# Longer transfers in a one-core graph-attention kernel: x by eight blocks, results by four, the last block of adj in halves

## The chip, the cores and the metric

The kernel runs on one core of one Trainium2 chip. The metric is the device time of one execution in microseconds; lower is better. A core has five engines that are named here as the profile names them: PE (TensorE, with its weight loads as PEld), DVE (VectorE), ACT (ScalarE), POOL (GpSimd) and SP (SyncE, which here only issues transfers). Sixteen DMA engines move data between HBM and the core's memory.

## The reference

`x` is 4096 x 512, `adj` 4096 x 4096, `W` 512 x 2048 (four heads of 512 columns) and `a` holds two vectors of 512 for each head; all are float32.

```python
def _L0_gnn_ref(h, adj_mat, W, a):
    N = h.shape[0]
    ht = (h @ W).reshape(N, N_HEADS, N_HIDDEN).transpose(1, 0, 2)
    a_src = a[:, :N_HIDDEN, 0]
    a_dst = a[:, N_HIDDEN:, 0]
    src = jnp.einsum('hnd,hd->hn', ht, a_src)
    dst = jnp.einsum('hnd,hd->hn', ht, a_dst)
    e = jax.nn.leaky_relu(src[:, :, None] + dst[:, None, :], SLOPE) + adj_mat[None]
    att = jax.nn.softmax(e, axis=-1)
    h_prime = jnp.einsum('hij,hjd->hid', att, ht)
    return h_prime.mean(axis=0)

x = _layernorm(x + _L0_gnn_ref(x, adj, L0_gnn_W, L0_gnn_a), axis=-1)
```

The entries of adj are zero or between 0.05 and 1e9, and they are added to the scores. Where the largest entry of a row stands far above all others, the softmax puts its whole weight on that one column, whatever the heads say. The row's result is then the layer norm of `x[i] + x[j] @ mean_of_heads(W)`, with j the column of the row's largest entry.

## The kernel before

`leading_rows` computes all rows in this short way and tests on the way whether it holds for each row. `general` computes blocks of rows in full, and is entered only where the test finds a row for which the short way doesn't hold. The order of the instructions is written by hand: each engine works off its own list in the order in which the code records it.

The rows are cut into 32 blocks (`NB`) of 128; block `ib` takes row `p * 32 + ib` on partition `p`, so that consecutive blocks of x or of the output are contiguous for each partition: one block of x or of the output is 2 KB per partition, four are 8 KB and eight are 16 KB. A block of adj is 2 MB, 16 KB per partition.

The loop over `t` (L423) starts one block at each turn and carries earlier ones further:

- `load_adj(t + 5)` (L117) issues the block of adj that comes five turns later, into a pool of six buffers. Blocks 28 to 30 come in two pieces and block 31 in four (`pieces`, L114). `load_x` (L124) issues several blocks of x at once into `hold`, which holds all of x and later the results. All these, and the stores, are issued by SP in one queue, in the order of the code.
- `segment_maxima(t, ...)` (L162) has DVE reduce the block to one maximum for each segment of 16 or 32 columns. A block up to 30 is reduced in two instructions, block 31 in four, one for each piece. Between the first and the rest stands `find_column(t - 2)` (L210) of the block two turns earlier. At the last turn `middle` (L431) is 1, so one quarter of block 31 stands ahead of `find_column(29)` and three behind it.
- `find_segment(t)` (L174) has DVE find the largest segment. POOL then fetches that segment of each row ("lead", L191) by an indirect DMA. `find_column` two turns later has DVE find the place inside it, POOL computes the column (L216), and POOL fetches that row of x ("y", L202) by another indirect DMA. For block 31 the column is searched in the whole row instead (`find_column_in_row`, L219).
- `turn(t - 3)` (L225) transposes y on PE and copies it by ACT; `products` (L239) multiplies it by the mean of the heads of W and `residual` (L233) adds x. ACT computes the statistics (L263), POOL the factor (L270), and ACT writes the result to `hold` (L275).

Blocks 24 to 27 (`BEHIND` = 24, `LATE` = 28) are handled apart: their products are put by (L253), their x is loaded last, and x is added behind the loop, for 24 to 26 by POOL (`add_x(nc.gpsimd, ...)`, L261). The place of these adds in POOL's list matters for what follows. It is, after the gather of y for block 29: the add of block 24; column and y of block 30; row and lead of block 31; the add of block 25; y of block 31; the add of block 26 (L486 to L491).

Where x is loaded: blocks 0 to 3 ahead of the loop, behind the issue of adj 4 (L136), 4 to 11 at turn 3, 12 to 15 at turn 11, 16 to 23 at turn 15 (L418), 28 to 31 ahead of adj 31, and 24 to 27 at turn 31, in two pieces of two blocks (L440). Stores (L328) all stand behind the loop: 0 to 7 by four blocks, 8 to 23 by two (L482 to L485), and, when the rest of the code has been recorded, 28 and 29 one by one, 24 and 25 together, 26 and 27 together, 30, and 31 (L540 to L542).

A DMA of SP's queue takes one of eight semaphores in turn, and its issue waits until an earlier DMA on that semaphore has landed.

Of the kernel before, what the change touches and what calls it, by code (L numbers as in the profile page):

```python
# [13 lines left out]
OP = mybir.AluOpType  # L14
AX = mybir.AxisListType
# [53 lines left out]
def leading_rows(ctx, tc, x, adj, W, a, out, ident, v, n_bad, any_bad):  # L69
# [8 lines left out]
    nc = tc.nc  # L78
    N, D = x.shape
    H = a.shape[0]  # L80
    KB, NB, S = D // P, N // P, N // E
    S_EARLY = N // E_EARLY
    AHEAD = 5
    Q = 4
    PIECES = 4
    LATE = NB - Q
    BEHIND = LATE - Q

# [23 lines left out]
    adj_t = {}  # L112

    def pieces(ib):  # L114
        return PIECES if ib == NB - 1 else 2 if ib >= LATE else 1

    def load_adj(ib):  # L117
        if 0 <= ib < NB:
            t = adj_t[ib] = adj_pool.tile([P, N], F32, name="adj_t")
            n = pieces(ib)  # L120
            for k in range(n):
                nc.sync.dma_start(t[:, ts(k, N // n)], adj_rows[ib][:, ts(k, N // n)])

    def load_x(lo, n):  # L124
        nc.sync.dma_start(hold[:, ds(lo, n), :], x_rows[:, ds(lo, n), :])

    def load_w(kb):
        nc.sync.dma_start(hold[:, ds(w_at + kb * H, H), :], w_blocks[:, kb])
# [3 lines left out]
        nc.scalar.dma_start(a_rows[ts(s, H), :], a[:, ts(s, D), :].rearrange("h d o -> h (d o)"))  # L132
    for kb in range(KB):
        load_w(kb)
        load_adj(kb + 1)
    load_x(0, Q)  # L136
    for ib in range(KB + 1, AHEAD):
        load_adj(ib)

# [20 lines left out]
    seg_of, at_of, lead_of, y_t, yt_of, o_ps = {}, {}, {}, {}, {}, {}  # L160

    def segment_maxima(ib, lo, hi):  # L162

        e = E_EARLY if ib < EARLY else E
        if lo == 0:
            seg_of[ib] = small.tile([P, N // e], F32, name=f"seg{e}", bufs=2)
        n = max(pieces(ib), 2)
        for k in range(lo * n // PIECES, hi * n // PIECES):
            nc.vector.tensor_reduce(  # L169
                seg_of[ib][:, ts(k, N // e // n)],  # L170
                adj_t[ib][:, ts(k, N // n)].rearrange("p (s e) -> p s e", e=e), axis=AX.X, op=OP.max,
            )

    def find_segment(ib):  # L174
        seg = seg_of.pop(ib)
        nc.vector.max(out=top[:, ib, :], in_=seg)
        at = at_of[ib] = small.tile([P, 8], U32, name="at")
        nc.vector.max_index(at, top[:, ib, :], seg)  # L178
        if ib < NB - 1:
            fetch_segment(ib)  # L180
# [29 lines left out]
    def find_column(ib):  # L210
        if ib < BEHIND:
            find_inner(ib)
        within = small.tile([P, 8], U32, name="within")
        nc.vector.max_index(within, top[:, ib, :], lead_of[ib])  # L214
        col = small.tile([P, 1], U32, name="col")
        nc.gpsimd.tensor_tensor(col, at_of.pop(ib), within[:, 0:1], op=OP.add)  # L216
        gather_rows(ib, col)
# [7 lines left out]
    def turn(ib):  # L225
        y = y_t.pop(ib)
        tp = psum.tile([P, KB, P], F32, name="tp", bufs=2)
        for kb in range(KB):
            nc.tensor.transpose(tp[:, kb, :], y[:, ts(kb, P)], ident)  # L229
        yt = yt_of[ib] = rows.tile([P, KB, P], F32, name="yt")  # L230
        nc.scalar.copy(yt, tp)  # L231

    def residual(ib):  # L233
        start = ib not in o_ps
        if start:
            o_ps[ib] = psum.tile([P, D], F32, name="o")
        nc.tensor.matmul(o_ps[ib], ident, hold[:, ib, :], start=start, stop=False)  # L237
# [11 lines left out]
    def row_norm(ib):  # L249
        sq = rows.tile([P, D], F32, name="sq")  # L250
        nc.scalar.activation(sq, hold[:, ib, :], AF.Square, accum_out=xx[:, ib : ib + 1])  # L251
# [18 lines left out]
    def rstd(i):  # L270
        nc.gpsimd.tensor_scalar(sd[:, i], sd[:, i], 1.0 / D, EPS, op0=OP.mult, op1=OP.add)
        nc.gpsimd.tensor_tensor(sd[:, i], sd[:, i], power[:, : i.stop - i.start], op=OP.pow)  # L272
        nc.gpsimd.tensor_mul(nm[:, i], nm[:, i], sd[:, i])
# [54 lines left out]
    def store(queue, lo, n):  # L328
        queue.dma_start(out_rows[:, ds(lo, n), :], hold[:, ds(lo, n), :])

    def mean_of_heads(kb):
        o = psum.tile([P, D], F32, name="o")
        for h in range(H):
            nc.tensor.matmul(o, ident, hold[:, w_at + kb * H + h, :], start=(h == 0), stop=(h == H - 1))  # L334
        nc.scalar.activation(w_sum[:, kb, :], o, AF.Copy, scale=1.0 / H)  # L335
# [5 lines left out]
    def turn_a():  # L341
        tp = psum.tile([P, KB, P], F32, name="tp", bufs=2)
        for k in range(KB):
            nc.tensor.transpose(tp[:, k, : 2 * H], a_rows[:, ts(k, P)], ident[: 2 * H, : 2 * H])
        nc.scalar.copy(at_d, tp[:, :, : 2 * H])

    def turn_w(kb, h):
        tp = psum.tile([P, KB, P], F32, name="tp", bufs=2)
        for k in range(KB):
            nc.tensor.transpose(tp[:, k, :], hold[:, w_at + kb * H + h, ts(k, P)], ident)  # L350
        wt = rows.tile([P, KB, P], F32, name="wt")
        nc.scalar.copy(wt, tp)  # L352
        return wt

    def head_vector(kb, h, wt):

        for k in range(KB):
            nc.tensor.matmul(  # L358
                pv[:, kb, h : 2 * H : H], wt[:, k, :], at_d[:, k, h : 2 * H : H],
                start=(k == 0), stop=(k == KB - 1),  # L360
            )

    def head_norms():
        nc.vector.tensor_copy(v, pv)
        vv = once.tile([P, KB, 2 * H], F32, name="vv")
        nc.vector.tensor_mul(vv, v, v)
        pn = psum.tile([P, KB, 2 * H], F32, name="px", bufs=1)
        nc.tensor.matmul(pn, ones, vv, start=True, stop=True)
        n2 = once.tile([P, 2 * H], F32, name="n2")
        nc.vector.tensor_reduce(n2, pn.rearrange("p k c -> p c k"), axis=AX.X, op=OP.add)  # L370
        nc.scalar.activation(n2, n2, AF.Sqrt)
        both = once.tile([P, H], F32, name="both")
        nc.vector.tensor_add(both, n2[:, :H], n2[:, H:])
        nc.vector.tensor_reduce(vn, both, axis=AX.X, op=OP.max)
# [40 lines left out]
        nc.vector.tensor_reduce(total, pg, axis=AX.X, op=OP.add)  # L415
        nc.vector.tensor_scalar(any_bad, total, -1.0, float(N), op0=OP.mult, op1=OP.add)

    x_at = {Q - 1: (Q, 2 * Q), 3 * Q - 1: (3 * Q, Q), 4 * Q - 1: (4 * Q, 2 * Q)}  # L418
    vectors = [(kb, h) for kb in range(KB) for h in range(H)]
    vectors_at = {t: 2 if t < 3 else 1 for t in range(1, 15)}  # L420
    COLUMN, PROJECT, STATS, FINISH = 2, 3, 4, 6
# [1 line left out]
    for t in range(NB):  # L423
        if t == NB // 2:
            tc.mark_branch_hint_location("general", engines=HINTED)
        if t in x_at:
            load_x(*x_at[t])
        if t + AHEAD == NB - 1:
            load_x(LATE, Q)
        load_adj(t + AHEAD)  # L430
        middle = 1 if t == NB - 1 else 2  # L431
        segment_maxima(t, 0, middle)
        if t >= COLUMN:
            find_column(t - COLUMN)
        segment_maxima(t, middle, PIECES)
        pair = FINISH <= t < BEHIND + FINISH and t % 2 == 0
        if pair:
            rstd(slice(t - FINISH, t - FINISH + 2))
        if t == NB - 1:
            for ib in (BEHIND, BEHIND + 2):  # L440
                load_x(ib, 2)
        find_segment(t)
        if t < 2:
            mean_of_heads(t)
        elif t == 2:
            mean_of_heads(2)
            mean_of_heads(3)
        if t == 0:
            turn_a()
        turned = [(*vectors[0], turn_w(*vectors.pop(0))) for _ in range(vectors_at.get(t, 0))]  # L450
        if t == 16:
            head_norms()
        ib = t - PROJECT
        if t == NB - 1:
            for late in range(LATE, NB):
                row_norm(late)
        if t == NB - 2:
            residual(LATE)
            residual(LATE + 1)
        if ib >= 0:  # L460
            turn(ib)
            if ib > BEHIND:
                products(ib - 1, KB - 1, KB)
            if ib < BEHIND:
                residual(ib)
        for some in turned:
            head_vector(*some)
        if ib >= 0:
            products(ib, 0, KB if ib < BEHIND else KB - 1)
        if t >= BEHIND + STATS:  # L470
            put_by(t - STATS)
        elif t >= STATS:
            stats(t - STATS)
            row_norm(t - STATS)
        if pair:
            finish(t - FINISH)
            finish(t - FINISH + 1)
# [1 line left out]
    for ib in range(BEHIND, LATE):  # L479
        row_norm(ib)  # L480
    nc.scalar.activation(xx, xx, AF.Sqrt)
    for ib in range(0, 2 * Q, Q):  # L482
        store(nc.sync, ib, Q)
    for ib in range(2 * Q, BEHIND, 2):
        store(nc.sync, ib, 2)  # L485
    add_x(nc.gpsimd, BEHIND)  # L486
    find_column(NB - 2)
    fetch_segment(NB - 1)
# [48 lines left out]
    moments(NB - 1)  # L537
    factor(NB - 1, shift=True)
    finish_in_halves(NB - 1)
    for ib, n in ((NB - 4, 1), (NB - 3, 1), (BEHIND, 2), (BEHIND + 2, 2), (NB - 2, 1)):  # L540
        store(nc.sync, ib, n)
    store(nc.sync, NB - 1, 1)  # L542

# [152 lines left out]
```

## Time and profile before

| what | us |
|---|---|
| median of 3 runs | 235.78 (235.51 to 236.39) |
| the profiled execution's own time | 235.65 |
| its span on the core | 234.1 |
| PE busy | 197.5 (84%) |
| DVE busy | 191.6 (82%) |
| ACT busy | 111.6 (48%) |
| POOL busy | 100.3 (43%) |
| bytes moved | 97.06 MB, mean 415 GB/s |
| share of the chain of waits on DMA | 48% |

The busy times are averages over the whole span; the stages at its beginning and end have other limits than the middle. Sizes of the transfers that SP issues, with the median time from issue to landing:

| transfer | count | KB each | us |
|---|---|---|---|
| adj | 28 | 2048 | 31.7 |
| adj | 6 | 1024 | 28.0 |
| adj | 4 | 512 | 19.7 |
| x | 2 | 2048 | 36.5 |
| x | 3 | 1024 | 27.8 |
| x | 2 | 512 | 15.5 |
| results | 2 | 1024 | 13.8 |
| results | 10 | 512 | 14.3 |
| results | 4 | 256 | 6.7 |

The time from issue to landing is long because the transfers queue up one behind the other. Beside SP's queue POOL issues 32 gathers of y (7.7 us from issue to landing in the median) and 32 of lead (6.3 and 5.9).

### The profile page before, as it was taken

How to read it: one execution, taken by the hardware profiler on the slowest of the kernel's cores; microseconds unless marked ns; L12 is line 12 of the kernel's file. 1: busy time of each engine (PE TensorE's matmuls, PEld its weight loads, DVE VectorE, ACT ScalarE, POOL GpSimd, SP SyncE). 2: the span in 40 equal slices, each digit the busy share in tenths (PEclk: the TensorE clock that was granted, in tenths of full speed). 3: DMA queues.
4: the chain of work that ended last, by engine and by line, in shares of the span. 5: the costliest groups of instructions: out<-in, count | busy, mean ns of one | idle time of the engine just before them, and what ended most of it. 6: DMA issues, size and time to landing. Idle time of an engine off the chain costs nothing.

```text
span 234.1 us, 2486 instructions
## 1 busy us (share of the span) xinstructions
PE 197.5 (84%) x683; PEld 101.6 (43%) x683; DVE 191.6 (82%) x300; ACT 111.6 (48%) x267; POOL 100.3 (43%) x212
## 2 busy tenths in 40 slices
PE   0198959999999699999999599859899967999980
PEld 0034525765656356555544144324333423344360
DVE  0566885589929999999789986999999999989871
ACT  2003012155665447475768264645564654187561
POOL 2022232415524464646443642646465464557400
PEclk9999778999999999999999979999999999999997
DMA  6999999999999999999999999999999999999994
GB/s 243 432 428 417 445 419 434 418 444 420 433 422 427 430 424 433 426 419 431 434 427 427 429 433 424 419 436 419 435 428 417 425 427 421 413 426 419 416 386 179
DMA packets 12977, 97.06 MB, mean 415 GB/s; under 512 B 2072, under 2 KB 2584, under 8 KB 7200
## 3 DMA queue, kind: packets, MB, share of 16 engines
q1 hardware_dynamic: 9360, 88.08, 89.0%
q0 software_dynamic: 3584, 8.77, 9.5%
q8 instruction: 6, 0.10, 0.2%
q14 instruction: 11, 0.09, 0.1%
q10 hardware_dynamic: 16, 0.02, 0.0%
HBM read 88.47 MB, written 8.39 MB: 414 GB/s over the span
## 4 chain that ended last, share of the span: by engine, by line
DMA 48%; POOL 19%; issue 17%; DVE 11%; PE 2%; ACT 0%; POOLq 0%; DVEq 0%; ACTq 0%; SPq 0%
DMA adj_t<-in_adj_dram 41%; DVE seg L169 8%; POOL y L202 6%; POOL lead L191 5%; DMA y<-in_x_dram,col 3%; DMA lead<-in_adj_dram,row 2%; POOL sd L272 2%; PE o L286 2%; DMA a_rows<-in_L_gnn_a_dram 1%; DVE col L222 1%; POOL row L185 1%; POOL start L198 1%; POOL col L216 1%; POOL lead_early L191 1%; DVE at L178 1%
## 5 line engine op out<-in xcount | busy, mean ns | idle before, releaser
L169 DVE TENSOR_REDUCE seg<-adj_t 128x128 f32<-128x2048 f32 (+2 forms) x66 | 145.4, 2207 | 29.0 <-DMA adj_t<-in_adj_dram 29.0
L244 PE MATMUL o<-w_sum,yt 128*128 128x512 f32 x248 | 116.0, 609 | 0.7 <-ACT yt L231 0.7
L244 PEld LDWEIGHTS o<-w_sum,yt 128*128 128x128 f32 x248 | 44.8, 193 | 53.9 <-issue 42.4
L231 ACT COPY yt<-tp 128x512 f32<-128x512 f32 x32 | 18.8, 587 | 45.8 <-PE tp L229 45.7
L202 POOL DMA_INDIRECT y<-in_x_dram,col x32 | 30.8, 961 | 16.5 <-POOL col L216 15.4
L334 PE MATMUL o<-hold,ident 128*128 128x512 f32 x32 | 20.9, 815 | 14.6 <-DMA hold<-in_L_gnn_W_dram 14.6
L229 PE MATMUL tp<-ident,y 128*128 128x128 f32 x128 | 19.7, 276 | 13.7 <-DMA y<-in_x_dram,col 13.7
L237 PE MATMUL o<-hold,ident 128*128 128x512 f32 x52 | 26.8, 600 | 0.0
L229 PEld LDWEIGHTS tp<-ident,y 128*128 128x128 f32 x128 | 14.4, 141 | 26.8 <-issue 25.5
L185 POOL TENSOR_TENSOR row<-at,first 128x1 uint32<-128x1 uint32 x32 | 6.0, 188 | 43.7 <-DVE at L178 43.3
L352 ACT COPY wt<-tp 128x512 f32<-128x512 f32 x16 | 9.2, 586 | 31.5 <-PE tp L350 31.5
L191 POOL DMA_INDIRECT lead_early<-in_adj_dram,row x18 | 18.1, 1008 | 8.9 <-POOL row L185 8.9
L216 POOL TENSOR_TENSOR col<-start,within 128x1 uint32<-128x1 uint32 x31 | 5.8, 188 | 36.0 <-DVE within L214 36.0
L251 ACT ACTIVATE sq<-hold 128x512 f32<-128x512 f32 x32 | 19.8, 619 | 0.0
L358 PEld LDWEIGHTS pv<-at_d,wt 128*128 128x128 f32 x128 | 16.3, 191 | 6.8 <-ACT wt L352 3.7
L334 PEld LDWEIGHTS o<-hold,ident 128*128 128x128 f32 x32 | 8.1, 265 | 25.1 <-issue 20.2
L335 ACT ACTIVATE w_sum<-o 128x512 f32<-128x512 f32 x4 | 2.4, 598 | 33.0 <-PE o L334 33.0
L277 ACT ACTIVATE hold<-o,nm,sd 128x512 f32<-128x512 f32 x24 | 17.2, 769 | 0.0
L191 POOL DMA_INDIRECT lead<-in_adj_dram,row x14 | 14.0, 1003 | 7.0 <-POOL row L185 7.0
L268 ACT ACTIVATE sq<-o,nm 128x512 f32<-128x512 f32 x24 | 16.5, 687 | 0.8
L358 PE MATMUL pv<-at_d,wt 128*128 128x2 f32 x128 | 15.3, 244 | 0.6 <-ACT wt L352 0.6
L266 ACT ACTIVATE sq<-o 128x512 f32<-128x512 f32 x24 | 14.6, 609 | 0.0
(91 smaller groups left out, 150.8 us busy)
## 6 DMA issues: line engine op xcount, KB each, us to landing
adj_t<-in_adj_dram SPq DMA_DIRECT2D x28, 2048.0 KB, 31.7
adj_t<-in_adj_dram SPq DMA_DIRECT2D x6, 1024.0 KB, 28.0
out_dram<-hold SPq DMA_DIRECT2D x10, 512.0 KB, 14.3
hold<-in_L_gnn_W_dram SPq DMA_DIRECT2D x4, 1024.0 KB, 18.8
hold<-in_x_dram SPq DMA_DIRECT2D x2, 2048.0 KB, 36.5
hold<-in_x_dram SPq DMA_DIRECT2D x3, 1024.0 KB, 27.8
adj_t<-in_adj_dram SPq DMA_DIRECT2D x4, 512.0 KB, 19.7
out_dram<-hold SPq DMA_DIRECT2D x2, 1024.0 KB, 13.8
```

The lines of the kernel that those rows point to most:

```text
L169: nc.vector.tensor_reduce(seg_of[ib][:, ts(k, N // e // n)], adj_t[ib][:, ts(k, N // n)].rearrange("p (s e) -> p s e", e=e), axis=AX.X, op ...
L191: nc.gpsimd.indirect_dma_start(out=lead, out_offset=None, in_=adj_segs_early if early else adj_segs, in_offset=bass.IndirectOffsetOnAxis(a ...
L202: nc.gpsimd.indirect_dma_start(out=y, out_offset=None, in_=x, in_offset=bass.IndirectOffsetOnAxis(ap=col[:, :1], axis=0),)
L229: nc.tensor.transpose(tp[:, kb, :], y[:, ts(kb, P)], ident)
L231: nc.scalar.copy(yt, tp)
L237: nc.tensor.matmul(o_ps[ib], ident, hold[:, ib, :], start=start, stop=False)
L244: nc.tensor.matmul(o_ps[ib], yt_of[ib][:, kb, :], w_sum[:, kb, :], start=(start and kb == 0), stop=(kb == KB - 1),)
L251: nc.scalar.activation(sq, hold[:, ib, :], AF.Square, accum_out=xx[:, ib : ib + 1])
L268: nc.scalar.activation(sq, o, AF.Square, bias=nm[:, i], accum_out=sd[:, i])
L277: nc.scalar.activation(hold[:, ib, :], o_ps.pop(ib), AF.Identity, bias=nm[:, i], scale=sd[:, i])
L334: nc.tensor.matmul(o, ident, hold[:, w_at + kb * H + h, :], start=(h == 0), stop=(h == H - 1))
L358: nc.tensor.matmul(pv[:, kb, h : 2 * H : H], wt[:, k, :], at_d[:, k, h : 2 * H : H], start=(k == 0), stop=(k == KB - 1),)
```

## The change

`PIECES` becomes 2, so block 31 of adj comes in two DMAs of 1 MB and is reduced in two instructions, one ahead of `find_column(29)` and one behind. x of blocks 0 to 23 comes in three DMAs of eight blocks: the first ahead of the issue of adj 4, the second at turn 7 and the third at turn 15. x of 24 to 27 is one DMA at turn 31. The results of 0 to 23 are stored by four blocks. 28 and 29 are stored together. SP issues 56 transfers in place of 65 for loads and stores of adj, W, x and results; the bytes are the same.

```diff
-    PIECES = 4
+    PIECES = 2
...
     def pieces(ib):
-        return PIECES if ib == NB - 1 else 2 if ib >= LATE else 1
+        return 2 if ib >= LATE else 1
...
     for kb in range(KB):
         load_w(kb)
+        if kb == KB - 1:
+            load_x(0, 2 * Q)
         load_adj(kb + 1)
-    load_x(0, Q)
...
-        n = max(pieces(ib), 2)
-        for k in range(lo * n // PIECES, hi * n // PIECES):
+        for k in range(lo, hi):
             nc.vector.tensor_reduce(
-                seg_of[ib][:, ts(k, N // e // n)],
-                adj_t[ib][:, ts(k, N // n)].rearrange("p (s e) -> p s e", e=e), axis=AX.X, op=OP.max,
+                seg_of[ib][:, ts(k, N // e // PIECES)],
+                adj_t[ib][:, ts(k, N // PIECES)].rearrange("p (s e) -> p s e", e=e), axis=AX.X, op=OP.max,
             )
...
-    x_at = {Q - 1: (Q, 2 * Q), 3 * Q - 1: (3 * Q, Q), 4 * Q - 1: (4 * Q, 2 * Q)}
+    x_at = {lo - 1: (lo, 2 * Q) for lo in range(2 * Q, BEHIND, 2 * Q)}
...
-        middle = 1 if t == NB - 1 else 2
-        segment_maxima(t, 0, middle)
+        segment_maxima(t, 0, 1)
         if t >= COLUMN:
             find_column(t - COLUMN)
-        segment_maxima(t, middle, PIECES)
+        segment_maxima(t, 1, PIECES)
...
         if t == NB - 1:
-            for ib in (BEHIND, BEHIND + 2):
-                load_x(ib, 2)
+            load_x(BEHIND, Q)
...
-    for ib in range(0, 2 * Q, Q):
+    for ib in range(0, BEHIND, Q):
         store(nc.sync, ib, Q)
-    for ib in range(2 * Q, BEHIND, 2):
-        store(nc.sync, ib, 2)
...
-    for ib, n in ((NB - 4, 1), (NB - 3, 1), (BEHIND, 2), (BEHIND + 2, 2), (NB - 2, 1)):
+    for ib, n in ((LATE, 2), (BEHIND, 2), (BEHIND + 2, 2), (NB - 2, 1)):
         store(nc.sync, ib, n)
```

## The prediction

> **What bounds the kernel now.** I read the share of the DMA engines first, by stage, then the last part of the chain of waits, then the rows of VectorE (DVE) and GpSimd (POOL) around the last block of adj.
>
> ```profile
> DMA  6999999999999999999999999999999999999994
> ```
>
> ```profile
> 2.00:20.00 18.00, 8.66 (x17) 3.73 (x18) 9.74 (x7) 1.89 (x3) 1.74 (x6) 1.00 1.00 416
> ...
> 182.00:208.00 26.00, 22.73 (x68) 10.00 (x69) 25.00 (x34) 13.60 (x32) 13.51 (x27) 1.00 1.02 422
> 208.00:222.00 14.00, 13.44 (x44) 5.97 (x42) 12.31 (x37) 9.97 (x29) 8.37 (x11) 1.00 1.02 419
> 222.00:228.00 6.00, 5.21 (x23) 3.65 (x22) 4.74 (x13) 3.78 (x7) 0.00 (x0) 1.00 0.97 385
> 228.00:234.10 6.10, 0.00 (x0) 0.00 (x0) 1.10 (x5) 0.86 (x2) 0.00 (x0) 0.79 0.48 190
> ```
>
> The first line is the page's DMA row over 40 slices. The window rows give start and end, length, busy us of PE, its weight loads, DVE, ACT and POOL, the clock, then the DMA share and GB/s. The 16 DMA engines are full from 3 us to 225 us (shares of 1.00 to 1.02); only the last 9 us have room. Up to the landing of adj's last piece the time is bytes over rate.
>
> ```profile
> 215.40 7.09 DMA y<-in_x_dram,col
> ...
> 222.62 0.63 PE tp L229 x4
> ...
> 224.11 3.55 PE o L286 x16
> ...
> 229.11 0.56 ACT hold L326
> ```
>
> The chain ends with block 31: its gather of rows of x, turn, product, norm, done at 229.67; the store behind it is issued at 229.70. The landing records of the queue's semaphores say when it is over: on 15 DMA engines that store lands between 231.53 and 231.86, on the sixteenth at 232.84. That engine lags: its earlier landings are 228.81 (block 29), 230.04 (24 and 25), 231.29 (26 and 27), 231.97 (30), spaced at 1.23, 1.25 and 0.68, which is its own transfer time. So it worked without a break, and the end (span 234.10) is set by it, 0.98 us behind the others. Its lag was 0.35 until 219.8. There an 8 KB packet of the instruction queue starts (220.23, 309 ns), and the two 4 KB packets after it took 368 and 487 ns where 159 is usual. The compute chain therefore has about 1.0 us of cover.
>
> ```profile
> 203.37 1.20 DVE L169 TENSOR_REDUCE seg<-adj_t 128x32 f32<-128x1024 f32 x1
> ...
> 207.51 1.22 DVE L169 TENSOR_REDUCE seg<-adj_t 128x32 f32<-128x1024 f32 x1 [0.15 <-DMA adj_t<-in_adj_dram]
> ...
> 209.88 0.09 DVE L214 MATCH_VALUE_LOAD within<-top,lead 128x8 f32 x1 [0.35 <-DMA lead<-in_adj_dram,row]
> ...
> 210.21 4.42 DVE L222 FIND_INDEX8 col<-top,adj_t 128x8 uint32<-128x4096 f32 x1
> ```
>
> ```profile
> 208.75 1.27 POOL L261 TENSOR_TENSOR adj_t<-adj_t,hold 128x512 f32<-128x512 f32 x1 [1.86 <-ACT sq L251]
> ...
> 211.01 0.97 POOL L202 DMA_INDIRECT y<-in_x_dram,col  x1 [0.60 <-POOL col L216]
> ...
> 215.40 0.96 POOL L202 DMA_INDIRECT y<-in_x_dram,col  x1 [0.67 <-issue]
> ```
>
> The first quarter of block 31 is reduced at once, the last when it lands (207.49). POOL's add at L261 is put down to ACT, but its semaphore instruction lasts to 208.5, when x of 24 and 25 lands (208.54): it is that DMA.
>
> **Two rules of the skill.** The Trainium skill, "DMA: Bandwidth & Descriptors", Rules for kernel authors, asks for at least 1 MiB per DMA and for small ones to be joined. Here the gain is small: packets of 4 KB per partition move at 419 GB/s (208 to 222 us), those of 16 KB at 430. "Perfetto Trace Analysis", DMA Optimizations, says that a split lets work start sooner where the DMA engines are mostly idle. Here they are full, yet the split of block 31 does feed DVE earlier: a wait of 0.15 us, then a piece of 1.22 and not of 2.27. The forecast goes by the rows.
>
> **The change, part by part.**
>
> *x of 0 to 23 by eight.* The two DMAs of 1 MB and two of 2 MB become three of 2 MB, at other places in SP's queue. Against before, adj 4 has 2 MB more ahead of it, 5 to 7 have 1 MB more, 8 to 11 1 MB less, 12 to 15 1 MB more, 16 and later the same. 1 MB is 2.44 us at 430 GB/s. So block 4 is late by 4.9 us and 12 to 15 by 2.4. What hides it: the engines stay full, bytes ahead of adj 20 are equal, and DVE waits there for 2.98 us (at 142.79), more than the 0.3 that it would still be late at block 16 (116.2 for 115.90, at 5.66 us a block from block 12's landing at 93.5). PE is the fuller engine here (6.06 us a block, turning block 6 at 80.77 after a wait of 1.80), and blocks 8 to 11 come earlier for it. x of 8 to 15 lands behind adj 11 (85.56 - 2.44 + 5.2 = 88.3); its first reader, block 8's residual, is at 93.4 now and 91.9 then. Cost 0 (no gain either, since the engines are full in both orders); if that cover failed, 2.4 us.
>
> *Fewer packets.* By rates (430 for 16 KB, from the page's GB/s slices at 6 to 12 us; 425 for 8 KB, from windows between 180 and 196; 419.5 for 4 KB): 2.44, 2.467 and 2.50 us per MB. x to 23: 2 MB at 0.027; adj 31: 2 MB at 0.03; x of 24 to 27: 1 MB at 0.03; results 8 to 23: 4 MB at 0.03; 28 and 29 half a MB at 0.03. Sum about 0.3 us, of which 0.1 is ahead of adj's last landing. The stores are never starved on either side: with eight queue slots, the one that a store waits for is that of the eighth DMA before it, and landings show those done.
>
> *Block 31 in halves.* DVE is ready at 203.37; now quarter 0 is there (202.91). A half is complete with quarter 1, at 204.2. Its reduction then takes 2.27 (the row of 128x2048), to 206.5. Block 29's index, which stands behind it, moves from 204.86 to 206.5, and so its gather from 205.93 to about 207.5. The second half lands at 207.4, is reduced to 209.65 (208.73 now), and 0.80 later the maximum's place is known: 210.45. The wait for the lead of block 30 (to 209.79) is now covered, which takes 0.35 off. The search of 4.42 ends at 215.2 instead of 214.63: +0.5.
>
> *x of 24 to 27 at once.* The add at L261 waits for the whole MB, which lands where 26 and 27 did (209.85) less 0.2: start 209.85, +1.1. Behind it on POOL stand block 30's column and gather (211.01 to 211.9), block 31's row and lead gather (212.46 to 213.35), the next add (to 215.6 instead of 214.72) and block 31's gather: 215.6 + 0.67 = 216.3. That is +0.9 and more than what DVE asks for, so this is the binding one.
>
> *The gathers beside longer packets.* Issue to landing of the y gathers has a median of 8.1 us at 132 to 169 us (16 KB packets beside them), 6.6 at 179 to 191 (8 KB), and 6.1 to 7.1 after 200 (mostly 4 KB; the 7.09 is the one that met the instruction packet, and had 15 engines done at 6.35). The stores now have 8 KB packets: +0.3 to +0.5, so block 31's rows land at 222.9 if no instruction packet meets them, 223.9 if one does.
>
> *PE.* Block 29's turn moves from 213.01 to 214.35 (gather at 207.5 plus 6.65, and 0.15). Little of PE's row is idle until 222.19, so it ends at about 223.5. Block 31's turn starts at the later of the two, 223.5 to 224.0 (222.62 now). I take +1.2; bounds +0.4 (POOL's delay alone, no packet met) and +2.2 (both, and a full 16 KB-like latency).
>
> *The end.* All behind the turn shifts by 1.2: last store issued at 230.9. A free engine lands it 1.83 to 2.16 later, as now: 233.06 at most. The lagging engine ends block 30 at 231.97 - 0.3 = 231.7, so it is waiting by then. 233.06 for 232.84: +0.2. Joining 28 and 29 puts 28's store back from 217.3 to 29's 222.1, inside a full queue; it costs 0.
>
> Sum: 235.65 (the profiled execution, 1.55 around its span) + 0.2, with 0.1 more should an instruction packet lie on the last store's engine again: 235.95. The median of the runs shown is 0.13 higher, so 236.1.
>
> **The rivals.**
>
> 1. *No cover (slower).* Block 31's chain is put back by 2.2 us or more. Mechanism: POOL's in-order queue behind the one add, with gathers slowed by 8 KB packets and by an instruction packet. At 2.5 the last store is issued at 232.2, lands at 234.4, +1.5: 237.3. For it: four delays of the same sign, on engines that are 90% full (12.31 and 13.44 of 14 us). Against: they overlap, the larger counts and not the sum. It decides from 2.2, where cover (1.0) and the 1.2 us below are used up.
> 2. *The bytes decide (faster).* The chain is late by 0.4 only, the last store is issued at 230.1 and lands at 232.3, -0.5: 235.3; without a disturbed engine a little less. For it: the queue is the bound for 222 us. Against: savings are 0.3 us.
> 3. *The early reordering isn't absorbed.* The 2.4 us of blocks 12 to 15 stay: 238.2. Against: equal bytes at block 20.
>
> That the change doesn't do what it says is no rival: SP's list in the built program has the longer transfers at these places.
>
> **How the numbers follow.** Forecast 0.58, rival 1 0.26, rival 2 0.11, rival 3 0.05. What a measurement of this kernel can tell from no change is about 0.5%, 1.2 us. Faster by more: only rival 2 with a free last engine, 0.06. Slower by more: rival 1 nearly whole, rival 3, and 0.02 of the forecast: 0.33. Same: 0.61. The range takes rival 2's 235.3 with 0.1 for its free engine, and most of rival 1: 235.2 to 237.5. The forecast's own range (+0.4 to +2.2 on the chain) is 235.3 to 236.9.
>
> **What would show it.** Right: DMA share still 1.0 until 225; a DVE wait of some 0.8 us ahead of block 31's first half, then two pieces of 2.27; L261's first add at about 209.9; block 31's gather issued at 216.0 to 216.6; its turn at 223.5 to 224. Wrong: an issue before 215.6 or after 217.5, DMA share under 0.98 anywhere before 220, PE waiting for x near block 8, or DVE meeting block 20 later than 143.3.

## The result, and the profile after

The changed kernel takes 236.30 us in the median of 22 runs, the kernel before 235.56 in the median of 22 runs taken beside it (one of these took 1136.14 us, which a median hardly feels). The ratio is 1.0031, with a 95% interval from 1.0019 to 1.0044. It is slower by 0.3%; the interval leaves out zero as well as the 0.5% named in the prediction. Medians, here and below, leave out one run of one kernel (243.15 us, results by eight blocks), which fell in a slower state of the chip. The profiled execution took 236.19 us with a span of 234.5 (235.65 and 234.1 before).

First the page's DMA row of the changed kernel over 40 slices, then its windows (start and end, length, busy us of PE, its weight loads, DVE, ACT and POOL, the clock, the DMA share, GB/s).

```profile
DMA  6999999999999999999999999999999999999974
```

```profile
182.00:208.00 26.00, 22.11 (x64) 9.44 (x63) 24.25 (x32) 13.15 (x31) 13.29 (x27) 1.00 1.01 424
208.00:222.00 14.00, 11.96 (x42) 5.81 (x42) 11.23 (x34) 10.10 (x29) 7.33 (x9) 1.00 1.01 425
222.00:228.00 6.00, 6.00 (x24) 3.81 (x23) 5.36 (x15) 3.74 (x9) 1.27 (x3) 1.00 0.79 324
228.00:234.50 6.50, 0.95 (x5) 0.49 (x3) 1.85 (x6) 1.22 (x3) 0.00 (x0) 0.77 0.53 211
```

Up to 222 us the DMA engines are as full as before. In the next 6 us they are not: the share falls from 0.97 to 0.79 and the rate from 385 to 324 GB/s. PE, which had slack there (5.21 us busy of 6), is now busy for all of it and for 0.95 us more behind 228. The stores no longer end last because the queue is full; they end last because the compute chain hands them over late.

The end of the chain of waits of the changed kernel (start, length, what; "..." leaves out short pieces):

```profile
212.99 6.64 DMA lead<-in_adj_dram,row
...
219.66 0.20 DVE inner L208
...
221.12 0.22 PE px L409 x2
221.34 2.77 PE o L244 x6
224.11 0.44 PE tp L229 x4
...
230.41 0.56 ACT hold L326
```

Before, the transfer ahead of block 31's turn in this view was the gather of its rows ("y", 215.40 for 7.09 us). Now it is the fetch of its lead segment, issued at 212.99 and landed at 219.63. Block 31's own column doesn't need the lead; the test of whether the short way holds for its rows does. The test runs on DVE from 219.66; a count of its outcome (L409) and most of block 30's products stand in PE's list ahead of block 31's turn. From the landing of the lead to the turn it takes 4.32 us. PE waits for the count only briefly, as its row shows (in brackets the wait):

```profile
221.12 0.22 PE L409 MATMUL px<-gap,ones 128*1 128x32 f32 x2 [0.32 <-DVE gap L405]
```

From block 29's turn (214.79) to this wait PE works without a gap. So two paths lie close together: without the wait, PE's own work since block 29's turn would have let block 31's turn start at about 223.63, an estimate (223.95 less 0.32).

The DVE and POOL rows of the changed kernel (start, us, engine, line, operation, and in brackets the idle time before it with what ended it):

```profile
204.05 2.29 DVE L169 TENSOR_REDUCE seg<-adj_t 128x64 f32<-128x2048 f32 x1 [0.75 <-DMA adj_t<-in_adj_dram]
...
206.96 2.29 DVE L169 TENSOR_REDUCE seg<-adj_t 128x64 f32<-128x2048 f32 x1 [0.45 <-DMA adj_t<-in_adj_dram]
...
210.27 4.42 DVE L222 FIND_INDEX8 col<-top,adj_t 128x8 uint32<-128x4096 f32 x1
```

```profile
207.31 0.96 POOL L202 DMA_INDIRECT y<-in_x_dram,col  x1 [0.54 <-POOL col L216]
209.84 1.27 POOL L261 TENSOR_TENSOR adj_t<-adj_t,hold 128x512 f32<-128x512 f32 x1 [1.57 <-DMA hold<-in_x_dram]
...
211.54 0.97 POOL L202 DMA_INDIRECT y<-in_x_dram,col  x1 [0.27 <-POOL col L216]
...
215.46 0.96 POOL L202 DMA_INDIRECT y<-in_x_dram,col  x1 [0.21 <-PE tp L229]
```

Halves: the first half is met after a wait of 0.75 us, block 29's gather goes out at 207.31 (205.93 before), but the search in block 31 ends where it did (214.69; before 214.63). x of 24 to 27 at once: the first add starts at 209.84 (208.75), block 30's gather at 211.54 (211.01), block 31's lead fetch at 212.99 (212.46). Block 31's gather goes out at 215.46, 0.06 later than before. Its turn starts at 223.95 (222.62), its store is issued at 231.00 (229.70): the chain is 1.30 us late, and the end 0.44. From the last store's issue to the end of the span it is 3.5 us now and was 4.4 before.

Sixty us earlier nothing is amiss: DVE meets block 20 at 142.61 after a wait of 2.11 us, and PE's weight loads wait for x only once, for 0.6 us (0.7 before).

### The profile page after: what moved, and what is told of

It reads as the page before. It is cut to its first block, busy times and chain, and to the rows that moved or that the text cites. A ratio compares the mean times of both kernels' runs of the same rounds, so it can differ in the third digit from the quotient of the medians.

```text
span 234.5 us, 2467 instructions
## 1 busy us (share of the span) xinstructions
PE 197.6 (84%) x683; PEld 101.5 (43%) x683; DVE 191.4 (82%) x298; ACT 111.9 (48%) x267; POOL 100.3 (43%) x212
## 4 chain that ended last, share of the span: by engine, by line
DMA 72%; DVE 21%; PE 3%; issue 1%; ACT 0%; SPq 0%; DVEq 0%
DMA adj_t<-in_adj_dram 69%; DVE seg L169 16%; DMA lead<-in_adj_dram,row 3%; PE o L244 2%; PE o L286 2%; DVE col L222 1%; DVE at L178 1%; DVE top L176 1%; DVE within L214 1%; DVE inner L208 0%; ACT hold L326 0%; DVE halves_st L320 0%; PE tp L229 0%; SPq L128 0%; SPq L122 0%
## 5 line engine op out<-in xcount | busy, mean ns | idle before, releaser
L169 DVE TENSOR_REDUCE seg<-adj_t 128x128 f32<-128x2048 f32 (+1 forms) x64 | 145.3, 2272 | 29.9 <-DMA adj_t<-in_adj_dram 29.7
L334 PE MATMUL o<-hold,ident 128*128 128x512 f32 x32 | 20.8, 811 | 14.6 <-DMA hold<-in_L_gnn_W_dram 14.6
L237 PE MATMUL o<-hold,ident 128*128 128x512 f32 x52 | 27.4, 613 | 0.0
```

What stands on the lines that cost most here:

```text
L169: nc.vector.tensor_reduce(seg_of[ib][:, ts(k, N // e // PIECES)], adj_t[ib][:, ts(k, N // PIECES)].rearrange("p (s e) -> p s e", e=e), axi ...
```

## The experiments

In the expectations, A is the account that block 31 in halves puts back block 29's gather and turn, and PE carries that to block 31's turn; B that the one transfer of x of 24 to 27 puts back POOL's add and so block 30's gather and block 31's lead fetch; C that the longer stores slow the gathers beside them. "Cover" is the time by which the chain can be late before the end moves. Each time below is a median, with the median of the kernel before, measured beside it; "chain" is the issue of the last store in the profile less 229.70.

**Block 31 in quarters again** (the rest as changed):

```diff
-    PIECES = 2
+    PIECES = 4
...
-        segment_maxima(t, 0, 1)
+        middle = 1 if t == NB - 1 else 2
+        segment_maxima(t, 0, middle)
```

> The changed kernel with block 31 of adj in quarters again, one ahead of block 29's column and three behind; all else as changed. Theory A (the half-size piece holds back block 29's column and gather on DVE, and PE's turn of 29 carries it to the end): block 29's gather issued at about 205.9 and not 207.3, its turn at 213.0 to 213.4 and not 214.8, last store issued at 229.6 to 230.0 and not 231.0; time 235.2 to 235.6, at or under the kernel before. Theory B (POOL's add for block 24 behind the 1 MB transfer of x): last store still at 230.6 or later, time 236.0 to 236.3. Theory C (gathers slowed by 8 KB packets of the stores): the turn of 31 stays at 223.5 or later, 236.0.

235.86 us against 235.54, ratio 1.0018 (1.0006 to 1.0029). Block 29's turn is back at 213.17, as A has it, but block 31's comes at 223.73, only 0.22 sooner than in the changed kernel. The chain of waits of this kernel:

```profile
213.07 6.34 DMA lead<-in_adj_dram,row
...
220.90 0.22 PE px L410 x2
...
223.89 0.44 PE tp L230 x4
```

The lead fetch holds block 31's turn although block 29 is on time. A is not the whole cause.

**Halves alone, on the kernel before:**

```diff
-        return PIECES if ib == NB - 1 else 2 if ib >= LATE else 1
+        return 2 if ib >= LATE else 1
...
-        middle = 1 if t == NB - 1 else 2
+        middle = 2
```

> The kernel before with block 31 of adj in halves alone, one half ahead of block 29's column. Theory A: nearly the whole of the change: last store issued at 230.8 to 231.2, time 236.0 to 236.4, ratio 1.002 to 1.004. B and C: 235.5 to 235.8, last store at 229.7 to 230.2.

235.67 against 235.54, 1.0011 (0.9996 to 1.0027). The chain of waits of this kernel shows what A describes, PE without a gap from block 29's turn to block 31's:

```profile
207.61 6.74 DMA y<-in_x_dram,col
...
214.48 0.63 PE tp L229 x4
...
220.67 2.77 PE o L244 x6
223.44 0.44 PE tp L229 x4
```

The chain is 0.63 us late, yet the time hardly moves. A's mechanism is real; its price was wrong, since beside short stores nearly all of it is covered.

**Block 29's column ahead of both halves:**

```diff
-        segment_maxima(t, 0, 1)
+        if t < NB - 1:
+            segment_maxima(t, 0, 1)
         if t >= COLUMN:
             find_column(t - COLUMN)
-        segment_maxima(t, 1, PIECES)
+        segment_maxima(t, 0 if t == NB - 1 else 1, PIECES)
```

> The changed kernel, but at the last turn block 29's column stands ahead of both halves of block 31. DVE then waits for lead of block 29 until 204.7, where the first half is there at 204.05. Theory A: block 29's gather is issued at 205.7, its turn at about 213.1; both halves end 0.3 later (209.6), the column search of 31 at 215.0, so block 31's turn starts at about 223.2; last store at 230.2 to 230.5; time 235.5 to 235.9, under the changed kernel by 0.4 to 0.8. B and C: as the changed kernel, 236.2 to 236.5.

236.12 against 235.54, 1.0022 (1.0011 to 1.0033). Block 29's gather goes out at 206.01 and its turn is at 213.41, but DVE now waits for block 29's lead instead, as its row shows:

```profile
204.94 0.09 DVE L214 MATCH_VALUE_LOAD within<-top,lead 128x8 f32 x1 [1.50 <-DMA lead<-in_adj_dram,row]
```

Block 31's turn stays at 223.89, 4.31 behind its lead's landing at 219.58. With A's path out of the way, the lead's is left, as with the quarters.

**x of 24 to 27 in two again** (the rest as changed):

```diff
-            load_x(BEHIND, Q)
+            for ib in (BEHIND, BEHIND + 2):
+                load_x(ib, 2)
```

> The changed kernel with x of 24 to 27 in two transfers of 512 KB again. Theory A: POOL's first add comes 1.1 earlier (208.7), but block 31's gather follows the column search on DVE by 0.77 in both profiles, so it stays at 215.4 to 215.6, and block 30's rows are not waited for; last store at 230.9 to 231.1; time 236.1 to 236.4. Theory B: last store at 229.9 to 230.2, time 235.3 to 235.7.

235.75 against 235.54, 1.0015 (1.0000 to 1.0029). The first add starts at 208.57, the lead lands at 219.03, block 31's turn is at 223.34. Much of the loss is gone, as B has it, but not all: the last store is issued at 230.39, between the two forecasts, and the lead fetch still takes 6.35 us from its issue (5.25 before). The chain of waits is now A's, PE without a gap from block 29's turn to block 31's:

```profile
214.50 0.63 PE tp L229 x4
...
220.51 0.22 PE px L409 x2
220.73 2.77 PE o L244 x6
223.50 0.44 PE tp L229 x4
```

The lead's landing plus the usual 4.31 us comes to 223.34 too, so here the two paths end together.

**One spare DVE instruction in the last chain**, on either kernel:

```diff
     stats_of_half(NB - 1, 1)
+    spare = small.tile([P, nc.vector.BN_STATS_DIM], F32, name="spare", bufs=1)
+    nc.vector.bn_stats(spare, hold[:, 0, :])
     moments(NB - 1)
```

> The kernel before with one more instruction on DVE in the last chain, between the statistics of block 31's second half and their joining: a bn_stats of 128x512 (0.69 us in the profile) whose result nobody reads. Cover theory (the last DMA engine's stream ends 0.98 us behind the others in the profile of before, so the chain has that much to spare): last store issued at 230.4, time 235.5 to 235.8, at most 0.25 over before. Theory of no cover: 236.1 to 236.3, +0.6 to +0.7.

> The changed kernel with the same spare bn_stats in its last chain. The change has used up what there was to spare: cover theory says the whole 0.69 shows, less at most 0.2: last store at 231.7, time 236.7 to 237.0, against 236.3 for the changed kernel. No cover in either kernel: the same +0.7 here. A cover that is still there: +0.2 or less.

On the kernel before: 236.15 against 235.64, 1.0038 (1.0024 to 1.0051), so 0.51 us for a chain 0.32 us later. On the changed one: 237.37, 1.0073 (1.0048 to 1.0097), about 1.0 us more than without the spare instruction, for a chain 0.74 later (231.74 for 231.00). Both lost more than the chain's delay, against the cover. The traces show one difference. Each kernel ends with two 8 KB packets of the instruction queue; they start 1.67 us or more behind the last store's issue in the kernel before and in the changed one, but 1.04 us behind it in both runs with the spare instruction, among that store's packets. On the kernel before they took 700 and 498 ns (309 ns each without the spare instruction), and the store landed at 232.73 and 233.37 on the last two engines when the first was done at 231.86. On the changed kernel they took 587 and 593 ns (309 and 378 without), and the store landed 1.85 to 2.81 us behind its issue (1.84 to 2.22 without). From the last store's issue to the end it takes 4.6 us (4.1 in the other). Whether the added instruction moved these packets wasn't tried.

**The same test without an added instruction:** on the kernel before, a later place for block 30's factor and norm, not needed there so early:

```diff
     stats_of_half(NB - 1, 0)
+    stats_of_half(NB - 1, 1)
     factor(NB - 2)
     normalise(NB - 2, o_ps.pop(NB - 2))
-    stats_of_half(NB - 1, 1)
```

> The kernel before, with no instruction more or less: block 30's factor and normalisation (0.13 and 0.55 us on DVE) stand behind the statistics of block 31's second half instead of ahead of them, so that they lie in the last chain. Chain +0.75: last store issued at 230.4, block 30's at 228.9. Cover theory (the run with a spare instruction lost 0.5 because two instruction packets, which took 700 and 498 ns, fell on the last store's DMA engine, and not because there was no cover): 235.5 to 235.8. No cover: 236.1 to 236.4.

235.57 against 235.60, 1.0001 (0.9985 to 1.0017). Its profiled execution took 236.19, 0.6 above its median, and was already 1.03 us late at block 29's gather, so its times aren't compared with the others. Within it, though, the last store is issued 7.60 us behind block 31's turn, for 7.08 in the kernel before: the edit does put the end of the chain back, by about 0.5 and not the 0.75 expected. The time stayed, as the cover says.

**The one transfer of x of 24 to 27 alone, on the kernel before** (the edit as in the change's diff):

> The kernel before with x of 24 to 27 in one transfer alone. Block 30's gather is issued at about 211.6 and lands 6.2 to 6.5 later beside 4 KB packets: turn of 30 at 218.0 to 218.2, of 31 at 222.8 to 223.3. If the end of before has 0.7 to spare, as with the halves alone (+0.13): 235.6 to 235.9. If the transfer costs what it costs beside the longer stores (+0.66): 236.1 to 236.3.

235.58 against 235.60, 0.9999 (0.9985 to 1.0013). The first add starts at 210.01, and the chain of waits of this kernel is the changed kernel's in small:

```profile
213.17 5.82 DMA lead<-in_adj_dram,row
...
220.47 0.22 PE px L409 x2
```

The chain is 0.65 us late, and it costs nothing.

**The longer stores alone, on the kernel before** (stores of 8 to 23 by four, 28 and 29 together, as in the change's diff):

> The kernel before with the stores alone as changed (8 to 23 by four blocks, 28 and 29 together). Theory C (gathers run beside 8 KB packets of stores take about 1.1 us longer than beside 4 KB: y of block 30 took 7.3 to 7.4 in the three profiles with stores by four and a single x, 6.2 to 6.4 with stores by two): lead of 31 takes 6.3, y of 30 and 31 take 7.1 to 7.4, turn of 30 at 218.2 to 218.5 and of 31 at 222.9 to 223.3; time 235.5 to 235.8. If packet size doesn't matter: turns at 217.5 and 222.6, and a queue that drains 0.15 earlier: 235.2 to 235.5.

235.10 against 235.64, 0.9982 (0.9967 to 0.9997): faster than the kernel before, and more than expected. Block 30's gather and block 31's lead fetch do take longer, 6.88 and 5.99 us for 6.16 and 5.25, as C has it. The chain is 0.24 late, but the end follows the last store's issue by 3.6 us and not by 4.4. Its windows:

```profile
208.00:222.00 14.00, 12.69 (x41) 5.81 (x40) 11.38 (x37) 9.80 (x27) 8.22 (x11) 1.00 1.02 425
222.00:228.00 6.00, 5.84 (x24) 3.65 (x22) 5.13 (x13) 3.78 (x7) 0.15 (x1) 1.00 0.91 373
```

425 GB/s for 419 from 208 to 222, and a share below 1 behind it: the queue is worked off a little earlier. The stores by four and the joined store of 28 and 29 weren't tried apart.

**x of 0 to 23 by eight and the longer stores**, without the other two parts (quarters, and x of 24 to 27 in two, put back in the changed kernel):

> The changed kernel with both of its early consumers' transfers as before: block 31 in quarters and x of 24 to 27 in two; x of 0 to 23 and the stores as changed. Theory of two parallel paths (halves put back block 29's turn, the 1 MB of x puts back block 30's; taking out one leaves the other): turn of 29 at 213.1, of 30 at 218.2 to 218.5, of 31 at 222.9 to 223.3; time 235.4 to 235.7, at least 0.2 under both single undos (235.86 and 235.75). If the two add up instead of standing side by side, 235.2 to 235.3; if neither matters beside the stores, 235.8 to 236.0.

235.20 against 235.64, 0.9974 (0.9966 to 0.9982). Beside the stores alone that is no difference, so x by eight costs and brings nothing that can be told. The turns of 29, 30 and 31 (212.80, 218.13 and 222.84) are those of two parallel paths: with only one of the two parts undone, block 31's turn had stayed at 223.73 or 223.34. The time lies 0.2 under what that account gave.

**Results of 0 to 23 by eight blocks, on the kernel before** (16 KB packets):

```diff
-    for ib in range(0, 2 * Q, Q):
-        store(nc.sync, ib, Q)
-    for ib in range(2 * Q, BEHIND, 2):
-        store(nc.sync, ib, 2)
+    for ib in range(0, BEHIND, 8):
+        store(nc.sync, ib, 8)
```

> The kernel before with the results of 0 to 23 stored by eight blocks, 16 KB packets. Twice the dose of theory C. If the gathers slow down with the packets beside them: y of 30 takes 8.0 to 9.0 (6.2 with 4 KB, 6.9 to 7.4 with 8 KB), lead of 31 7.0 or more, turn of 30 at 219.0 to 220.0, of 31 at 224.0 to 225.0, time 236.0 to 237.0. If it was something else than the packets: turns within 0.3 of those of the stores by four, time 234.9 to 235.3.

238.93 (five runs, 237.25 to 240.54) against 235.60, 1.0118 (1.0069 to 1.0167): slower than expected. Block 30's gather (the one that POOL issues between 210.5 and 215), first in the kernel before, then with the longer stores alone, then here:

```profile
DMA to landing us min/median/max: 6.2/6.2/6.2
```

```profile
DMA to landing us min/median/max: 6.9/6.9/6.9
```

```profile
DMA to landing us min/median/max: 8.5/8.5/8.5
```

The gathers slow down with the stores' packets: mostly 4 KB in the kernel before (from 211 to 218 us its queue moves 358 packets of 4 KB and 127 of 8 KB), then 8 and 16 KB. In this profile the lead of block 31 lands at 224.14, its turn is at 228.45, and from 222 to 228 the DMA share is 0.56: the engines idle, waiting for results. Not all of that is the stores' doing. The profiled execution, 240.54, is the slowest of the five, and DVE starts on block 31 at 205.32 without a wait, 1.95 later than in the kernel before; it had fallen behind by about that much before the first of these stores was issued at 198.46. That delay is in the turns; a time from issue to landing is counted from its own issue.

**The add of block 24 behind block 30's gather and block 31's lead fetch**, in the changed kernel with quarters:

```diff
-    add_x(nc.gpsimd, BEHIND)
     find_column(NB - 2)
     fetch_segment(NB - 1)
+    add_x(nc.gpsimd, BEHIND)
     add_x(nc.gpsimd, BEHIND + 1)
```

> The changed kernel with block 31 in quarters and x of 24 to 27 still in one transfer, but POOL's add of block 24 stands behind the column and gather of block 30 and the fetch of block 31's lead. If the 1 MB transfer costs its 0.66 (235.86 for 235.20) through POOL's list, the cost goes: block 30's gather issued at 210.6 to 210.9, turn of 30 at 217.6 to 218.0, of 31 at 222.7 to 223.0, time 235.0 to 235.3, level with the best so far. If it costs it in another way (as a transfer, or through ACT): 235.7 to 236.0.

236.09 (235.37 to 237.27) against 235.60, 1.0020 (1.0006 to 1.0034): no gain over the quarters alone. The lead lands at 218.64, 0.78 sooner than there, and block 30's turn comes 0.93 sooner, as meant. But the two adds now run together ahead of block 31's gather on POOL:

```profile
213.09 2.50 POOL L262 TENSOR_TENSOR adj_t<-adj_t,hold 128x512 f32<-128x512 f32 x2
215.75 0.96 POOL L203 DMA_INDIRECT y<-in_x_dram,col  x1 [0.16 <-issue]
```

That gather lands at 223.23 and holds block 31's turn (223.36). The profiled execution took 235.50, among the shortest of a wide scatter, so the 236.09 isn't explained by it; this run settles no more than that the wait moved.

All kernels side by side. Turn of 31, issue of the last store and end of the span are from the profiles; the last column is the median less that of the kernel before, measured beside it. "Held by" names the latest of three: y's landing plus 0.14, the lead's landing plus 4.31, and PE's work without a gap since block 29's turn.

| kernel | turn of 31 | held by | last store | end | end less store | median change |
|---|---|---|---|---|---|---|
| before | 222.62 | y of 31 | 229.70 | 234.10 | 4.40 | |
| + halves | 223.28 | PE since 29 | 230.33 | 234.00 | 3.67 | +0.13 |
| + x of 24 to 27 at once | 223.30 | lead of 31 | 230.35 | 234.11 | 3.76 | -0.02 |
| + longer stores | 222.86 | y of 31 | 229.94 | 233.54 | 3.60 | -0.54 |
| + longer stores, x by eight | 222.84 | y of 31 | 229.91 | 233.59 | 3.68 | -0.44 |
| these two + halves | 223.34 | PE since 29 and lead of 31 | 230.39 | 234.05 | 3.66 | +0.21 |
| these two + x of 24 to 27 at once | 223.73 | lead of 31 | 230.78 | 234.30 | 3.52 | +0.32 |
| all (after) | 223.95 | lead of 31 | 231.00 | 234.54 | 3.54 | +0.74 |

In the two kernels with y behind the longer stores the lead comes only 0.15 to 0.21 sooner, and the profile's chain goes by it.

Two parts of the table are the finding. With short stores the span ends at 234.0 to 234.1 whether the last store is issued at 229.70 or at 230.35. With long ones it ends some 3.6 us after that issue, wherever it falls (4.1 with the spare instruction). The longer stores thus gain half a microsecond and take away the cover; after that, halves cost 0.65 (+0.21 for -0.44), the transfer of x 0.76, and both 1.18, less than their sum of 1.41, as fits two paths side by side. The ratios of these rows have intervals of 0.1 to 0.2% to either side, 0.2 to 0.4 us, so neither that difference nor the one between 0.65 and 0.76 is clear of the noise. On short stores each cost about nothing. Both together on short stores weren't tried; that the cover would have been too small for them is likely, since each alone already brings the end within 3.7 or 3.8 us of the last store's issue, but it isn't shown. The change as a whole is the gain of about -0.5 plus these 1.2.

The versions with the longer stores and neither of the two other late parts are faster than both kernels: 0.9982 (0.9967 to 0.9997) and 0.9974 (0.9966 to 0.9982) of the kernel before.

## Why the prediction was right, and which of its steps were not

The forecast of 236.1 and of no change beyond 0.5% held, with its two main sizes: the chain late by 1.3 (forecast 1.2), the end by 0.44 in the profiles (0.2 to 0.3), most of the delay taken by the cover. A free queue landed the last store 1.84 to 2.22 us behind its issue (forecast 1.83 to 2.16). That 236.1 came so near to 236.30 is in part luck: by medians the change cost 0.74 where the forecast added 0.3, but it started from 235.78, the median of three runs, which lies 0.22 above that of the 22. The road to these numbers was only partly the one described, and one of the forecast's own signs of being wrong came: block 31's gather was issued before 215.6. One of its signs of being right didn't: the DMA share doesn't stay at 1.0 until 225, but is 0.88 from 222 to 225.

- *The early reordering cost nothing*: right, by block 20's wait and by the run with x by eight and long stores against long stores alone.
- *Block 31 in halves*: right up to block 29's gather (207.31 for 207.5) and turn (214.79 for 214.35). Wrong at its end: the second half landed at 206.93 and not at 207.4, so the search ended 0.06 late and not 0.5.
- *x of 24 to 27 at once*: the add's start was right (209.84). The step that failed is what the forecast called "the binding one", block 31's gather at 216.3; it came at 215.46. The 0.67 us of "issue" ahead of that gather had been taken as a cost that follows the add. It follows DVE's search: 214.63 to 215.40 before, 214.69 to 215.46 after, 0.77 each time, while the add ahead ended at 214.73 and 215.25. (Where the add ended at 215.43, with x of 24 to 27 at once on short stores, the gather followed it by 0.16.) The same error is in block 30's gather, forecast 0.9 late and 0.53 late in fact: a gap of 0.60 shrank to 0.27 when the engine in front was the later one.
- *What holds block 31's turn*: forecast as block 29's turn, carried by PE to 223.5, or the gather of y. PE's path was right, at about 223.63; it is beaten by 0.32 us by the lead of block 31, which the forecast costed only to its issue (213.35, measured 212.99) and whose landing it never followed to its reader, the test and the count in PE's list. The lead had 0.60 us of slack before (landing 217.71 plus 4.31 is 222.02, turn 222.62), and its landing moved by 1.92: 0.53 at the issue and 1.39 in flight. In the halves-alone run, and with x in two again, the forecast's path does hold.
- *Gathers beside longer packets*: right in kind, mis-sized. Forecast +0.3 to +0.5. Measured +0.72 for block 30's gather and +0.74 for the lead fetch from the stores alone, +1.23 and +1.39 in the changed kernel. By luck this made up for the POOL delay that didn't come: PE's path alone gives a chain 1.0 late, the slow lead fetch the other 0.3. The last two are 0.5 to 0.65 above those of the stores alone; x of 24 to 27 at once adds about as much on short stores too (6.58 and 5.82 us, +0.42 and +0.57). Why it does is open: the transfer has landed before these gathers are issued. They are issued 0.5 to 0.7 later than in the kernel before, and each figure is from one profile.
- *Fewer packets, 0.3 us*: a right sign, too small. The stores alone gained 0.54, with the queue worked off sooner and the last engine less far behind (it lands block 30's store at 231.60 for 231.97, and the last store 0.34 behind the other engines for 0.98). The packet rates explain at most the 0.15 expected for these stores; the 419 GB/s read for 4 KB was of a mix, in which 8 KB packets were about a quarter (211 to 218 us). The rest is open. And the full queue in which joining 28 and 29 was to cost nothing wasn't there in the changed kernel: from 222 the engines have room, while the joined store is issued at 224.06.
- *The cover of about 1.0 us*: shown by three runs in which a chain late by 0.63 and 0.65 (profiles) or put back by an edit of the last steps (by about 0.5) costs 0.13, -0.02 and -0.03. So some 0.65 of it is shown. Whether more was there isn't: with the chain that late, the end already follows the last store by 3.7, about as with the longer stores. It isn't a constant: the spare instruction lost 0.51 for 0.32 of delay, and it goes with the short stores whose queue makes it.

Of the rivals, the first had the right place (POOL's list, slow gathers) and too large a delay; the second, that the bytes decide, is what the longer stores do alone; the third has no trace.

## What to carry to other kernels

When a full DMA queue covers a late compute chain, a change that relieves the queue also takes the cover away: cost the other edits as if they were bare, and try each part with and without the relief. For each transfer put back, follow every reader in every engine's list, the check or count in the middle as well as the one that ended the chain before; its slack, here 0.60 us, is what decides. An idle gap ahead of an instruction is no cost to be carried along with the instruction in front; find first what it follows by laying two occurrences side by side.

## What the runs showed of the hardware

- The time of a small gather depends on the packets of the plain transfers beside it, at the same share of the engines: 6.16, 6.88 and 8.5 us for gathers of y beside stores of mostly 4, of 8 and of 16 KB per packet, and 5.25, 5.99 and 8.35 us for the lead fetch. The Trainium skill, "DMA: Bandwidth & Descriptors", Queues, rings and completion order, says that each DMA engine takes turns among its queues packet by packet. The sign agrees with that, since a turn then lets a longer packet go first. The size isn't explained by one turn: a lead fetch is 16 packets of 1 KB for 16 engines and lost 0.74 us, where a packet of 8 KB takes 0.15 us longer than one of 4 KB (309 and 159 ns). No run here shows the turns themselves.
- Longer isn't always faster. The same page's Rules for kernel authors asks for 1 MiB or more; here results by 1 MB, with 28 and 29 joined, gained 0.5 us, and those by 2 MB lost 3.3 in the median and 1.7 in the best run, so the measurement, not the rule, sets the size.
- Instruction packets share the DMA engines. In the changed kernel two of 8 KB start 1.67 us behind the last store's issue, and that store's landing is spread over 0.38 us (232.84 to 233.22). With the spare instruction they start 1.04 us behind it, and the landing is spread over 0.96 us (233.59 to 234.55), for a first landing equally far behind the issue.
